# A gated cross-attention and mixture-of-experts layer: 512-byte table entries, written by token column, and a table cleared in five pieces from ScalarE's queue

## The chip, the cores and the metric

The kernel runs on one core of one Trainium2 chip. The metric is the device time of one execution in microseconds (us). The time before is the median of three runs. Beside them stands one profiled execution, from which all durations and waits are read.

## The reference, cut to what matters

There are 8 batches of 512 tokens with 256 features, so 4096 tokens. A layer norm and a masked cross-attention with 16 heads are added to `x` through a tanh gate. Then each token is normalised again, sent to its two best of eight experts, and their outputs, weighted by the router's probabilities, are added through a second gate.

```python
x = x + jnp.tanh(g_xattn[0]) * _L0_xattn_ref(_layernorm(x), ctx, ctx, mask, ...)
# the feed-forward part, on the result:
probs = jax.nn.softmax(x_flat @ router_w + router_b, axis=-1)
top_w, top_idx = jax.lax.top_k(probs, 2)
for e in range(8):
    h = jax.nn.gelu(x_flat @ expert_up[e].T, approximate=False)
    output = output + comb[:, e:e+1] * (h @ expert_down[e].T)
x = x + jnp.tanh(g_ffn[0]) * output
```

## The kernel before

The kernel computes only the chosen experts. It keeps a table in DRAM that lists, expert by expert, which tokens an expert has to process. `LINES` is 300 lines of 128 entries, 38,400 entries in all. An entry holds three numbers that matter (`FIELDS = 3`: the token to write to, the token to read from, its weight) and is padded to `ENTRY` 32-bit words, 16 before, so 64 bytes.

**Clearing.** `clear_table` (L158) fills a tile in SBUF with empty entries (three memsets on GpSimd, L161 to L163) and writes it over the whole table with one DMA from SyncE's queue (L165): 1536 pieces of 1600 bytes, 2400 KB. In the path that this input takes (`attend_near`) it is called at step `b == -1` (L1214) with a tile of tag "raw".

**The steps of the attention part.** `attend_near` goes through `b` from -1 to 7. In step `b` it computes the attention of batch `b` (`weights_T`, `weigh`: matmul, exponential on ScalarE, matmul), finds the score maxima of batch `b + 1` (`find_tops`), projects and normalises what comes next (`project`: `n_xnT`, `k`, `q` on ScalarE), and finishes batch `b - 1`. Each step has four groups `g` with three positions `n`; the dictionary `plan` says which piece of work goes where.

**Entering.** For every batch, `place` (L366) works out on GpSimd where in the table each token of the batch goes. It also fills `entries[:, b % 2]` for all four token columns and both choices at once: one copy (L391) and one multiplication (L394). Then `enter(t)` (L399) issues two indirect DMAs (L401), one for each choice of token column `t`; that is 8 per batch and 64 in all. There are two such buffers, so the entries of a batch may be overwritten once the DMAs of the batch two before have landed.

**The experts.** A job takes up to 256 rows of one expert. `list_rows` (L807) reads two table lines from DRAM, `fetch` (L843) gathers the token rows with indirect DMAs on GpSimd (`xg`), `turn` transposes them, `go_up` and `go_down` do the matmuls, `fetch_y` gathers the rows of the output that exist already (`y`), and L903 scatters the sum back to `out`. The first four jobs run inside steps 5 to 7; the others follow the attention part, and the last two batches' entries are made among them.

**What sets the order.** Each engine works through its own queue in order, but the order of a queue is not the order of the code. The program is built by a scheduler that follows the dependencies and lets an instruction whose inputs are ready go ahead of earlier written ones that still wait. `tc.keep_in_program_order(ins)` pins one instruction behind whatever was written last for its engine. Most vector and many ScalarE instructions carry such a pin; the instructions of `clear_table` and of `enter` do not. Every DMA issued from SyncE or ScalarE takes one of eight completion semaphores in turn and waits, on the engine that issues it, for the semaphore's last user.

The places that the change and the prediction name: `entries` L154, `clear_table` L158, `place` L366, `enter` L399, `plan_pairs` L672 with its line L686, `load_x` L89, `load_window` L510, the step loop L1209, and `attend_anywhere` (the path not taken here).

Of the kernel before, what the change touches and what calls it, by code (L numbers as in the profile page):

```python
# [11 lines left out]
F32 = mybir.dt.float32  # L12
# [8 lines left out]
P = 128  # L21
# [30 lines left out]

LINES = E * SHARE + 2 * SIZES[3]

ENTRY = 16
FIELDS = 3
JOBS = [(k, n) for k in range(2) for n in range(SIZES[k])]
for _n in range(OFTEN):
# [10 lines left out]
def flamingo_layer(ctx: ExitStack, tc: tile.TileContext, a: dict, out: bass.AP):  # L69
# [6 lines left out]
    def fixed(shape, name, dtype=F32):  # L76
        return const.tile(shape, dtype, tag=name, name=name)
# [73 lines left out]
    tokens_i = fixed([P, B * QT], "tokens_i", I32)  # L151
    nc.gpsimd.iota(tokens_i, pattern=[[P, B * QT]], base=0, channel_multiplier=1)

    entries = fixed([P, 2, QT, 2, ENTRY], "entries", I32)  # L154
    nc.gpsimd.memset(entries, 0)
    place_i = fixed([P, B * QT, 2], "place_i", I32)

    def clear_table(t):  # L158

        many = t.rearrange("p (n c) -> p n c", c=ENTRY)[:, : LINES // 12]  # L160
        nc.gpsimd.memset(many, 0)  # L161
        nc.gpsimd.memset(many[:, :, 0], TOKENS)
        nc.gpsimd.memset(many[:, :, 1], TOKENS - 1)  # L163
        n = many.shape[1]
        nc.sync.dma_start(  # L165
            out=table.rearrange("(p r n) c -> p r (n c)", p=P, n=n),
            in_=t[:, : n * ENTRY].unsqueeze(1).to_broadcast([P, LINES // n, n * ENTRY]),
        )


    lower = fixed([P, E + 1, E], "lower")
# [88 lines left out]
    def shared(p2, small, bank):  # L260
# [40 lines left out]
        def finish(b):  # L301

            x2T = p2.tile([P, DC, S], F32, tag="xnT", name=f"x2T{b}", bufs=1)
            said = {}

            def t3(name, dtype=F32):
                return small.tile([P, QT, E], dtype, tag=name, name=f"{name}{b}", bufs=2)

            def t2(name):
                return small.tile([P, QT], F32, tag=name, name=f"{name}{b}", bufs=2)  # L310

            def keep_rows(xn):
                nc.sync.dma_start(out=token_rows(rows, b), in_=xn)

            def keep_x():
                nc.sync.dma_start(out=token_rows(out, b), in_=xs[b])

            def logits():

                ps = bank(f"route_ps{b}")[:, :P]  # L320
                for dc in range(DC):
                    for t in range(QT):
                        nc.tensor.matmul(
                            ps[32 * t : 32 * t + 32, :], lhsT=rw[:, dc, :], rhs=x2T[:, dc, t * P : (t + 1) * P],
                            start=(dc == 0), stop=(dc == DC - 1),
                        )
                said["lgT"] = small.tile([P, P], F32, tag="lgT", name=f"lgT{b}", bufs=1)
                nc.scalar.copy(said["lgT"], ps)

            def route():  # L330
                ps = bank(f"lg_ps{b}")[:, :P]
                nc.tensor.transpose(ps, said["lgT"], ident)
                said["lg"] = t3("lg")
                nc.vector.tensor_tensor(
                    said["lg"], ps.rearrange("p (t e) -> p t e", t=QT)[:, :, :E], over_t(rb), ALU.add
                )

            def choose():
# [24 lines left out]
                nc.vector.tensor_tensor(both, picks[:, :, 0, :], picks[:, :, 1, :], ALU.add)  # L363
                said["top"], said["picks"], said["both"] = top, picks, both

            def place():  # L366

                both = said["both"].rearrange("p t e -> p (t e)")
                ps = bank(f"place_ps{b}")
                n = QT * E  # L370
                nc.tensor.matmul(ps[:, :n], lhsT=before, rhs=both, start=True, stop=True)
                nc.tensor.matmul(ps[:, n : 2 * n], lhsT=ones, rhs=both, start=True, stop=True)
                counts = small.tile([P, 2, QT, E], F32, tag="counts", name=f"counts{b}", bufs=2)
                nc.scalar.copy(counts.rearrange("p i t e -> p (i t e)"), ps[:, : 2 * n])
                place = t3("place")
                for t in range(QT):
                    nc.gpsimd.tensor_tensor(place[:, t, :], counts[:, 0, t, :], filled, ALU.add)
                    nc.gpsimd.tensor_tensor(filled, counts[:, 1, t, :], filled, ALU.add)
                mine = slice(b * QT, (b + 1) * QT)
                at = small.tile([P, QT, 2], F32, tag="at", name=f"at{b}", bufs=2)  # L380
                picked = said["picks"]
                nc.gpsimd.tensor_tensor(
                    picked, picked, place.unsqueeze(2).to_broadcast([P, QT, 2, E]), ALU.mult
                )
                for k in (4, 2, 1):
                    nc.gpsimd.tensor_tensor(
                        at.unsqueeze(3) if k == 1 else picked[..., :k], picked[..., :k], picked[..., k : 2 * k],
                        ALU.add,
                    )
                entry = entries[:, b % 2]  # L390
                nc.gpsimd.tensor_copy(  # L391
                    entry[:, :, :, :2], tokens_i[:, mine].unsqueeze(2).unsqueeze(3).to_broadcast([P, QT, 2, 2])
                )
                nc.gpsimd.tensor_scalar(  # L394
                    entry.bitcast(F32)[:, :, :, 2], said["top"][:, :, :2], tg[:, 1:2], None, ALU.mult
                )
                nc.gpsimd.tensor_copy(place_i[:, mine, :], at)

            def enter(t):  # L399
                for i in range(2):  # L400
                    nc.gpsimd.indirect_dma_start(  # L401
                        out=table_parts[2 * t + i][:, :],
                        out_offset=bass.IndirectOffsetOnAxis(ap=place_i[:, t, i : i + 1], axis=0),
                        in_=entries[:, b % 2, t % QT, i, :], in_offset=None,
                    )

            places = [place] + [lambda t=t: enter(t) for t in range(b * QT, (b + 1) * QT)]
            return x2T, keep_x, keep_rows, logits, route, choose, places

# [224 lines left out]
    def experts(pool, seen, half_bank, bank, row_bank):  # L634
# [8 lines left out]

        def open_wide():
            wide.append(pool("wide", 1))

        def halves(s):
            return 3 if JOBS[s][0] == 2 else 2
# [318 lines left out]
                    some(middle, len(JOBS))  # L967

        plan_steps = [plan_full(0), plan_full(1), plan_rest]
        return plan_steps, open_wide, list_rows, fetch, load, turn, ups, fetch_y, downs, compute, compute_extra  # L970


    def attend_near(att):
# [6 lines left out]
        def bank(name):  # L980
            return ps_g.tile([P, 512], F32, tag="g", name=name)

        plans, open_wide, list_rows, fetch, load, turn_rows, ups, fetch_y, downs, compute, compute_extra = experts(
            pool, [b * S for b in (*PARTS, B)], lambda name: ps_s.tile([P, 512], F32, tag="s", name=name), bank,
            lambda name: ps_o.tile([P, 512], F32, tag="av", name=name),
        )
# [222 lines left out]
        for b in range(-1, B):  # L1209
# [1 line left out]
                load_x(b + 3, p2)  # L1211
                load_win(b + 3)
            if b == -1:
                clear_table(p2.tile([P, S], I32, tag="raw", name="none", bufs=1))  # L1214
            behind_route = list(later)
            later.clear()
            if b == 0:
# [13 lines left out]
                        plan[where].append(step)  # L1231
            for g in range(4):
                c, i = g // 2, g % 2
                if b >= 0:
                    pT = weights_T(b, c, i)
                work = deque(amid.get((b, g), []))
# [39 lines left out]
    def attend_anywhere(att):  # L1276
# [70 lines left out]
        for t in vals:  # L1347
            nc.gpsimd.memset(t[:, :, :, DH:], 1.0)
        load_ctx(0)
        clear_table(p2.tile([P, S], I32, tag="raw", name="none"))  # L1350

# [184 lines left out]
    with which.Else():  # L1536
        with ExitStack() as att:
            attend_anywhere(att)
        with ExitStack() as exp:
            pool = lambda name, bufs, **kw: exp.enter_context(tc.tile_pool(name=name, bufs=bufs, **kw))  # L1540
            ps_h, ps_g = pool("ps_h", 4, space=PSUM), pool("ps_e", 4, space=PSUM)
            plans, open_wide, list_rows, fetch, load, turn_rows, _, _, _, compute, compute_extra = experts(
                pool, [TOKENS] * (len(PARTS) + 1),
                lambda name: ps_h.tile([P, 512], F32, tag="h", name=name),
                *[lambda name: ps_g.tile([P, 512], F32, tag="e", name=name)] * 2,
# [57 lines left out]
```

## Time and profile before

| | |
|---|---|
| median of 3 runs | 787.48 us (787.28 to 788.8) |
| profiled execution | 819.79 us, its span 818.0 us |
| PE / DVE / ACT / POOL busy in the span | 755.2 / 409.0 / 261.7 / 312.3 us |
| DMA packets, bytes | 82728, 113.32 MB |
| table<-none (the clear), SyncE's queue | 1 issue, 2400 KB |
| table<-entries (the entering) | 64 indirect DMAs, 62.8 us of GpSimd |

Times are from the span's start. PE is the matrix engine, DVE the vector engine, ACT ScalarE, POOL GpSimd and SP SyncE; SPq and ACTq mark what the queue of SP or ACT itself executes, such as issuing a DMA. A number in brackets with an arrow is the idle time of the engine before an instruction and what ended it. The profiled execution is 32 us longer than the median of the timed runs (819.79 against 787.48).

### The profile page before, as it was taken

To read this page: it belongs to the slowest core of one execution; us is meant where nothing else is said; L and a number is where in the kernel's file an instruction comes from. 1 tells how busy PE (TensorE), PEld (TensorE's weight loads), DVE (VectorE), ACT (ScalarE), POOL (GpSimd) and SP (SyncE) were. 2 spreads that over 40 slices of the span, in tenths; PEclk is the share of its full clock that TensorE was granted. 3 is DMA by queue.
4 is the path that set the end of the run, shared out by engine and by line. 5 is a ranking of instruction groups with operands and counts; after the bars stand their busy time and mean duration, and the time that the engine had idled before them with its cause. 6 is when DMAs were issued, how large, how long until landed. Compare 5 with 4: busy or idle time off the path is not lost. (4 is left out here: it accounts for less than half of the span.)

```text
span 818.0 us, 11151 instructions
## 1 busy us (share of the span) xinstructions
PE 755.2 (92%) x3898; PEld 544.3 (67%) x3898; DVE 409.0 (50%) x1315; ACT 261.7 (32%) x491; POOL 312.3 (38%) x420
## 2 busy tenths in 40 slices
PE   8999988888898989998799999999999999999992
PEld 3544534334465646677488888888788788878872
DVE  8898894958573575532053453524343423523300
ACT  4665654544553535422211112121211221121110
POOL 2020133333536151636563444344443444344331
PEclk9999997987998999999899999999999999999997
DMA  5700110100572230157436557575754654655310
GB/s 165 264 2 33 58 53 30 53 4 28 197 282 93 78 120 14 54 158 246 157 113 208 210 192 243 171 249 179 246 174 151 212 199 152 194 205 179 99 52 25
DMA packets 82728, 113.32 MB, mean 139 GB/s; under 512 B 16605, under 2 KB 67552, under 8 KB 82656
## 3 DMA queue, kind: packets, MB, share of 16 engines
q1 hardware_dynamic: 70000, 85.16, 31.4%
q0 software_dynamic: 11840, 26.76, 9.9%
q8 instruction: 35, 0.57, 0.3%
q10 hardware_dynamic: 816, 0.53, 0.2%
q14 instruction: 37, 0.30, 0.1%
HBM read 92.66 MB, written 20.28 MB: 138 GB/s over the span
## 5 line engine op out<-in xcount | busy, mean ns | idle before, releaser
L879 PE MATMUL h_ps<-xT,up 128*128 128x256 f32 (+1 forms) x1024 | 248.0, 398 | 7.6 <-issue 3.8
L897 PE MATMUL o_ps<-down,hT 128*128 128x256 f32 x1088 | 242.4, 380 | 4.9 <-DVE y L900 4.9
L897 PEld LDWEIGHTS o_ps<-down,hT 128*128 128x128 f32 x1088 | 205.4, 190 | 40.2 <-DVE y L900 6.8
L879 PEld LDWEIGHTS h_ps<-xT,up 128*128 128x128 f32 x1024 | 195.3, 192 | 52.6 <-issue 9.3
L868 DVE STREAM_TRANSPOSE xT<-xg 32x128 f32<-32x128 f32 (+1 forms) x368 | 115.6, 314 | 179.3 <-DMA xg<-rows,listed 167.7
L883 ACT ACTIVATE hT<-h_ps 128x512 f32<-128x512 f32 (+1 forms) x144 | 82.0, 573 | 342.7 <-PE h_ps L879 321.3
L903 POOL DMA_INDIRECT out<-y,listed x68 | 68.5, 1007 | 157.9 <-DVE y L900 133.8
L831 POOL DMA_INDIRECT y<-out,listed x68 | 65.0, 956 | 80.9 <-DMA out<-y,listed 53.8
L1038 DVE TENSOR_REDUCE tops<-t_ps 128x4 f32<-128x512 f32 x128 | 79.4, 683 | 25.8 <-PE t_ps L1033 15.1
L831 POOL DMA_INDIRECT xg<-rows,listed x68 | 66.3, 975 | 40.7 <-issue 18.6
L1068 ACT ACTIVATE n_pT<-w_ps 128x512 f32<-128x512 f32 x128 | 67.4, 602 | 39.0 <-PE w_ps L1063 35.6
L401 POOL DMA_INDIRECT table<-entries,place_i x64 | 62.8, 982 | 20.7 <-issue 16.2
L900 DVE SCALAR_TENSOR_TENSOR y<-o_ps,listed,y 128x256 f32<-128x256 f32 x68 | 31.1, 481 | 75.5 <-PE o_ps L897 51.4
L1063 PE MATMUL w_ps<-ql,km 32*128 32x512 f32 x256 | 54.1, 686 | 0.0
L1015 POOL TENSOR_TENSOR x<-x,bo 128x1024 f32<-128x1024 f32 x8 | 18.8, 2348 | 67.5 <-DVE bo L1014 38.9
L1087 DVE STREAM_TRANSPOSE raw<-n_av 128x512 f32<-128x512 f32 x32 | 22.8, 711 | 42.3 <-PE n_av L1081 19.6
L1033 PE MATMUL t_ps<-k,q 32*128 32x256 f32 x512 | 40.6, 416 | 0.3 <-ACT k L560 0.3
L1081 PE MATMUL n_av<-n_pT,nv 128*32 128x512 f32 x256 | 37.4, 659 | 2.7 <-DVE xT L856 2.7
L1033 PEld LDWEIGHTS t_ps<-k,q 32*128 32x128 f32 x512 | 25.5, 190 | 17.2 <-issue 11.8
L573 PE MATMUL q_ps<-n_xnT,wqT 128*128 128x512 f32 x64 | 32.4, 632 | 0.9 <-ACT n_xnT L286 0.6
L1102 PE MATMUL proj_ps<-woT,oT 128*128 128x256 f32 x128 | 31.4, 387 | 0.0
L1102 PEld LDWEIGHTS proj_ps<-woT,oT 128*128 128x128 f32 x128 | 23.4, 190 | 8.6 <-DVE st_f_a L225 3.4
(220 smaller groups left out, 538.6 us busy)
## 6 DMA issues: line engine op xcount, KB each, us to landing
up<-in_upT SPq DMA_DIRECT2D x32, 1024.0 KB
down<-in_downT SPq DMA_DIRECT2D x32, 1024.0 KB
out<-x SPq DMA_DIRECT2D x8, 512.0 KB
rows<-xn_f SPq DMA_DIRECT2D x8, 512.0 KB
x<-in_x SPq DMA_DIRECT2D x7, 512.0 KB
table<-none SPq DMA_DIRECT2D x1, 2400.0 KB
xg<-rows,listed POOLq DMA_INDIRECT x68
y<-out,listed POOLq DMA_INDIRECT x68
```

The source lines that it names most:

```text
L401: nc.gpsimd.indirect_dma_start(out=table_parts[2 * t + i][:, :], out_offset=bass.IndirectOffsetOnAxis(ap=place_i[:, t, i : i + 1], axis=0) ...
L831: ins = nc.gpsimd.indirect_dma_start(out=dst, out_offset=None, in_=src[: seen[JOBS[s][0]], :], in_offset=bass.IndirectOffsetOnAxis(ap=list ...
L868: nc.vector.transpose(dst[32 * g : 32 * g + 32, i], src[32 * i : 32 * i + 32, g])
L879: nc.tensor.matmul(ps[:, i, :], lhsT=up[:, dc, (f + i) * P : (f + i + 1) * P], rhs=xT[:, dc, :], start=(dc == 0), stop=(dc == DC - 1),)
L883: nc.scalar.activation(made[s][:, f : f + m, :], ps, AF.Gelu)
L897: nc.tensor.matmul(ps, lhsT=hT[:, f, h * P : (h + 1) * P], rhs=down[:, f, :], start=(f == 0), stop=(f == FC - 1))
L903: ins = nc.gpsimd.indirect_dma_start(out=out_parts[h][:, :], out_offset=bass.IndirectOffsetOnAxis(ap=listed[:, n, h, 0:1], axis=0), in_=y[ ...
L1033: ins = nc.tensor.matmul(ps[j][:, u], lhsT=q[rows_j, c, t * P : (t + 1) * P], rhs=k[rows_j, c], start=True, stop=True)
L1038: nc.vector.tensor_reduce(top[:, 2 * tp : 2 * tp + 2, :].rearrange("p t (i x) -> p t i x", i=2)[:, :, :, 32 * j], ps[j], AX.X, ALU.max,)
L1063: ins = nc.tensor.matmul(ps[j], lhsT=km[rows_j, c, i, :], rhs=lowered[b, c][rows_j, i, :], start=True, stop=True)
L1068: nc.scalar.activation(pT[:, j, :], ps[j], AF.Exp)
L1102: nc.tensor.matmul(ps[:, t - ts[0], :], lhsT=outs[b, c][:, t * P : (t + 1) * P], rhs=w["woT"][:, c, :], start=(c == 0), stop=(c == DC - 1),)
```

## The change

The entries become 128 words (512 bytes), so the table grows from 2.46 to 19.66 MB. `entries` has one buffer for each of the two choices instead of two for whole batches, and the copy and the multiplication are made in `enter`, for one token column and one choice at a time. `clear_table` now returns six steps: one that fills the tile (4 entries to a partition, 2 KB) and five that each issue a DMA of 3.93 MB, 1920 pieces of 2 KB. In `attend_near` they go to ScalarE's queue: the fill and the first piece are written at step -1, and one further piece at the beginning of each of the four groups of step 0, ahead of `weights_T`. None of them is pinned. The tile has the tag "xT" of the experts' pool instead of "raw".

```diff
-ENTRY = 16
+ENTRY = P
...
-    entries = fixed([P, 2, QT, 2, ENTRY], "entries", I32)
+    entries = fixed([P, 2, ENTRY], "entries", I32)
...
-    def clear_table(t):
-
-        many = t.rearrange("p (n c) -> p n c", c=ENTRY)[:, : LINES // 12]
-        nc.gpsimd.memset(many, 0)
-        nc.gpsimd.memset(many[:, :, 0], TOKENS)
-        nc.gpsimd.memset(many[:, :, 1], TOKENS - 1)
-        n = many.shape[1]
-        nc.sync.dma_start(
-            out=table.rearrange("(p r n) c -> p r (n c)", p=P, n=n),
-            in_=t[:, : n * ENTRY].unsqueeze(1).to_broadcast([P, LINES // n, n * ENTRY]),
-        )
+    def clear_table(t, queue):
+
+        many = t.rearrange("p (n c) -> p n c", c=ENTRY)
+        n, steps = many.shape[1], 5
+        runs = LINES // n // steps
+        parts = table.rearrange("(p k r n) c -> p k r (n c)", p=P, k=steps, n=n)
+
+        def fill():
+            nc.gpsimd.memset(t, 0)
+            nc.gpsimd.memset(many[:, :, 0], TOKENS)
+            nc.gpsimd.memset(many[:, :, 1], TOKENS - 1)
+
+        def put(k):
+            queue.dma_start(out=parts[:, k], in_=t.unsqueeze(1).to_broadcast([P, runs, n * ENTRY]))
+
+        return [fill, *(lambda k=k: put(k) for k in range(steps))]
...
-                entry = entries[:, b % 2]
-                nc.gpsimd.tensor_copy(
-                    entry[:, :, :, :2], tokens_i[:, mine].unsqueeze(2).unsqueeze(3).to_broadcast([P, QT, 2, 2])
-                )
-                nc.gpsimd.tensor_scalar(
-                    entry.bitcast(F32)[:, :, :, 2], said["top"][:, :, :2], tg[:, 1:2], None, ALU.mult
-                )
                 nc.gpsimd.tensor_copy(place_i[:, mine, :], at)
 
             def enter(t):
                 for i in range(2):
+                    nc.gpsimd.tensor_copy(entries[:, i, :2], tokens_i[:, t : t + 1].to_broadcast([P, 2]))
+                    nc.gpsimd.tensor_scalar(
+                        entries.bitcast(F32)[:, i, 2:3], said["top"][:, t % QT, i : i + 1], tg[:, 1:2], None, ALU.mult
+                    )
                     nc.gpsimd.indirect_dma_start(
...
-                        in_=entries[:, b % 2, t % QT, i, :], in_offset=None,
+                        in_=entries[:, i, :], in_offset=None,
                     )
...
+        def no_token():
+            return gather.tile([P, S], F32, tag="xT", name="none", bufs=2).bitcast(I32)
...
             if b == -1:
-                clear_table(p2.tile([P, S], I32, tag="raw", name="none", bufs=1))
+                clear = deque(clear_table(no_token(), nc.scalar))
+                clear.popleft()()
+                clear.popleft()()
...
             for g in range(4):
                 c, i = g // 2, g % 2
+                if b >= 0 and clear:
+                    clear.popleft()()
                 if b >= 0:
                     pT = weights_T(b, c, i)
```

The remaining lines of the diff pass `no_token` out of `experts` and let the other path issue its six steps at once on SyncE's queue.

More of the change, by code (lines that the diff above doesn't have):

```diff
@@ L969, in experts @@
         plan_steps = [plan_full(0), plan_full(1), plan_rest]
-        return plan_steps, open_wide, list_rows, fetch, load, turn, ups, fetch_y, downs, compute, compute_extra
+        return plan_steps, no_token, open_wide, list_rows, fetch, load, turn, ups, fetch_y, downs, compute, compute_extra
     def attend_near(att):
@@ L981, in bank @@
             return ps_g.tile([P, 512], F32, tag="g", name=name)
-        plans, open_wide, list_rows, fetch, load, turn_rows, ups, fetch_y, downs, compute, compute_extra = experts(
+        plans, no_token, open_wide, list_rows, fetch, load, turn_rows, ups, fetch_y, downs, compute, compute_extra = experts(
             pool, [b * S for b in (*PARTS, B)], lambda name: ps_s.tile([P, 512], F32, tag="s", name=name), bank,
@@ L1349, in attend_anywhere @@
         load_ctx(0)
-        clear_table(p2.tile([P, S], I32, tag="raw", name="none"))
+        for step in clear_table(p2.tile([P, S], I32, tag="raw", name="none"), nc.sync):
+            step()
         mask_i = load_mask(p2)
@@ L1541, in flamingo_layer @@
             ps_h, ps_g = pool("ps_h", 4, space=PSUM), pool("ps_e", 4, space=PSUM)
-            plans, open_wide, list_rows, fetch, load, turn_rows, _, _, _, compute, compute_extra = experts(
+            plans, _, open_wide, list_rows, fetch, load, turn_rows, _, _, _, compute, compute_extra = experts(
                 pool, [TOKENS] * (len(PARTS) + 1),
```

## The prediction, made before the changed kernel was seen

> **What bounds the kernel now.** I read the page first (engines, slices, the chain that ended last), then, since the change acts early and on queues, the timelines of ACT and SP from 18 to 62 us, busy time by stretch, and POOL's timeline at each batch of table entries.
>
> ```profile
> PE 755.2 (92%) x3898; PEld 544.3 (67%) x3898; DVE 409.0 (50%) x1315; ACT 261.7 (32%) x491; POOL 312.3 (38%) x420
> PE  8999988888898989998799999999999999999992
> ```
>
> PE is busy nearly everywhere. What stops PE for some us is not made up later: no later slice has idle time to give back. In the chain that ended last PE holds 11%; the rest is out and y DMAs and POOL of the last jobs, far from this change. What matters is whether the edit stops something that feeds PE.
>
> ```profile
> 22.46 2.07 ACT L275 ACTIVATE xn_a<-x,shift_a,rstd_end_a 128x256 f32<-128x256 f32 x4
> 24.70 0.37 ACT L546 COPY kn<-kv_ps 128x256 f32<-128x256 f32 x1 [0.16 <-PE kv_ps L542]
> 24.96 0.48 ACT L547 ACTIVATE nv<-kv_ps,kept 128x256 f32<-128x256 f32 x1
> 26.50 1.07 ACT L286 COPY n_xnT<-xnT_ps_a 128x512 f32<-128x512 f32 x2 [1.05 <-PE xnT_ps_a L285]
> 29.50 1.50 ACT L560 ACTIVATE k<-k_ps,bks,half 128x128 f32<-128x128 f32 x4 [1.93 <-PE k_ps L554]
> 33.49 0.69 ACT L577 ACTIVATE q<-q_ps,bqs 128x512 f32<-128x512 f32 x1 [2.48 <-PE q_ps L573]
> 37.63 2.04 ACT L1068 ACTIVATE n_pT<-w_ps 128x512 f32<-128x512 f32 x4
> ```
>
> This is ACT in step -1. It waits for PE by 1 to 2.5 us at a time, and PE waits for what ACT delivers (n_xnT, k, q): a chain in lockstep. The short holes are where an early-ready ACT instruction can slip in.
>
> ```profile
> 19.40 0.66 SPq L165 DMA_DIRECT2D table<-none  x1
> 20.16 3.64 SPq L92 DMA_DIRECT2D x<-in_x  x1
> 24.07 1.84 SPq L512 DMA_DIRECT2D win<-in_ctxT  x1
> 26.02 1.67 SPq L92 DMA_DIRECT2D x<-in_x  x1
> 24.00:29.00 5.00, 5.00 (x44) 3.24 (x43) 4.31 (x8) 2.36 (x6) 0.00 (x0) 1.00 1.06 383
> 29.00:34.00 5.00, 4.89 (x32) 2.82 (x31) 5.00 (x10) 2.02 (x5) 0.00 (x0) 1.00 1.09 374
> 37.00:60.00 23.00, 22.76 (x156) 11.18 (x152) 19.49 (x57) 16.22 (x34) 4.69 (x2) 1.00 0.02 7
> ```
>
> The first four lines are SP's queue, the last three the stretches (columns: PE, PEld, DVE, ACT, POOL, clock, DMA share, GB/s). The clear moves at some 375 GB/s with all DMA engines full; from 37 to 60 us they are nearly idle. The issue of the clear itself took 0.66 us, but the issue of the x load behind it took 3.64 instead of the 0.38 that the same load takes with an empty queue (18.25). By the packet records, that issue ended when some 103 earlier pieces per DMA engine were outstanding, the four after it at 79 to 97. So an issue returns once about 100 pieces per engine or fewer lie ahead, and until then its engine stands still. For SP that costs nothing.
>
> ```profile
> L686 DVE TENSOR_SCALAR line<-iota_e x3: 163/165/174, 21.9 to 419.8; 128x9 f32<-128x9 f32 x3
> ```
>
> This unpinned line belongs to a plan whose next operations (L669, L709) run at 197 us. Its first execution is at 21.9: the build puts unpinned instructions whose inputs are ready into the first hole, 175 us ahead of their place in the code.
>
> **The change part by part.**
>
> *The clear on ACT.* A piece has 1920 parts of 2 KB, 120 per DMA engine; at 375 GB/s its 3.93 MB take 10.5 us, and all five 52. The pieces need only the fill on POOL (17.2 us before), so by the L686 row I expect pieces 1 to 4 not in the four groups of step 0 but in ACT's first holes of step -1, behind nv or n_xnT. Piece 0 is written before the pinned xn_a, so it stays ahead of it: at 22.5, 0.66 us. Its data start about 25[...] and share the engines with 2.5 MB of x and window loads, which begin at about 20.3 and no longer queue behind the clear. Piece 1, issued at about 26, returns once 20 parts per engine of piece 0 are through. Each further one returns a piece later: piece 4 when 480 - 100 = 380 parts per engine are done, 12.45 MB; with the loads 14.95 MB, or 39.9 us at 375 GB/s. That is 60 us. ACT makes n_xnT then instead of at 26.5: 34 us lost. Queued behind it are n_xnT, k, q and the exponentials of batch 0; PE stops at k_ps (28.75), as both banks that it could use hold n_xnT's inputs, and DVE stops after the tops it has been given. About 1 us comes back, since DVE's backlog is cleared: +33.
>
> Here a rule speaks to it. The Trainium skill, "DMA: Bandwidth & Descriptors", section "Issuing engines are not separate DMA queues", says that issuing from several engines adds no bandwidth and saves only issue time, which it calls usually small relative to the DMA. By the rule the five issues cost ACT 5 x 0.66 = 3.3 us and the sum would be some 6; by the row of 3.64 us it is 33. I take the row: the pieces are larger than what fits.
>
> *SP without the clear.* The x load at 20.16 goes out 0.7 us earlier and its data up to 7 us earlier. No early PE wait is on x, so 0. The "raw" tile is first needed at 44.5, long after the old clear: 0. Later loads share engines with the clear until about 80 us; of SP's there are one window at 39 and at 68 and the out store at 76.9, none near its deadline: 0, up to +1. ACT's own semaphore waits are for loads that are done by 28.
>
> *Entering.*
>
> ```profile
> 127.29 0.95 POOL L401 DMA_INDIRECT table<-entries,place_i  x1 [0.30 <-DMA table<-entries,place_i]
> 129.72 0.20 POOL L391 COPY entries<-tokens_i 128x16 int32<-128x16 int32 x1 [1.47 <-DMA table<-entries,place_i]
> 428.15 0.99 POOL L903 DMA_INDIRECT out<-y,listed  x1 [0.30 <-issue]
> 438.89 0.48 DVE L900 SCALAR_TENSOR_TENSOR y<-o_ps,listed,y 128x256 f32<-128x256 f32 x1 [1.03 <-DMA y<-out,listed]
> ```
>
> An indirect DMA takes 1.26 us of POOL with the gap, eight a batch 10.1. Now each has a copy (nearest row 0.20) and a multiplication (nearest 0.32 for 8 elements, I take 0.30) ahead, with 0.08 between: 0.66 more, 5.3 per batch, less the 0.5 removed: +4.8, in all 38 us of POOL's 818. The new wait: a copy may overwrite `entries[:, i]` only when the DMA of the column before has landed. The second line shows landing within 1.47 us of the last issue; the other choice's turn in between takes 1.9, so the wait is 0 with quiet DMA, and 1 to 3 us per column when weights stream (the y gathers in the chain land in 2.7 to 3.4). For batches 0 to 3 POOL has idle stretches of 5 us or more behind the entries. For batches 6 and 7 the out and xg DMAs stand behind them: the out at 428.15 went out when POOL got to it, and the y gather behind it arrived 1 us late for DVE (last line). Jobs alternate, so most of a 5 us delay is absorbed: between 0 and +10, I take +2.
>
> *512-byte entries.* The gain of wider writes can only be POOL's waits for landed entries, 6.5 us in five places, none of which PE waits for; `listed` reads the same 12-byte pieces, and POOL waits for them 10.6 us in two places. Bound -3 to +1, taken as 0.
>
> Sum: 33 + 2 = +35, on a profiled execution of 819.8. The stall is set by DMA bytes, not by the matrix clock, so it carries over whole to the median: 787.5 + 35 = 822.
>
> **The rivals.**
>
> *The pieces stay in their places* (one per group of step 0, near 37.5, 43, 50 and 57 us). Then piece 2 finds about 78 parts ahead and returns at once, piece 3 finds 116 and waits 1 us, piece 4 133 and waits 2.5. With 5 x 0.6 us of issue that is 6.5, of which ACT's holes there hide 1 to 2: +5, with entering +7: 794.5. For it: the code says so. Against: the L686 row.
>
> *An issue on ACT does not stop ACT*, or its queue holds more than SP's. Then 3 us of issue, mostly in holes, and the entering: +2, 789.5. Against: the first ACT activity comes right behind its three issues at the start.
>
> *Faster.* Nothing blocks, and the wider entries are listed sooner: the 2.4 and 8.2 us that POOL waits for `listed` shrink, and the 2.53 us that PE waits for xT at 371 goes. At most -3: 784.5. It decides only if ACT is stopped for under 1 us and POOL's extra 4.8 per batch are covered.
>
> *Not what it says:* if the build took the five pieces to overlap in the table, each would wait for the one before to land. The two weight loads into interleaved halves of `wkv` went out 0.4 us apart without such a wait, so I give it little; it would look like the first rival with waits of up to 12 us where ACT is early: +5 to +15.
>
> **How the numbers follow.** ACT blocked in step -1: 0.60, at 822, own range 812 to 831 (a piece or two in later holes saves up to 10, entering costs up to 8 more). Pieces in place or chained: 0.24, 790 to 803. No block: 0.11, 787 to 791. Faster: 0.05. The range 789 to 831 leaves out the faster case, half of "no block" and the tail of the first. 0.2% (1.6 us) is about what a measurement of this kernel can tell from no change; faster by more than that 0.05, within it 0.05, slower 0.90.
>
> **What would show it.** On ACT's queue five issues of table<-none between 22 and 60 us, three of some 10 us each; n_xnT of step -1 at about 60; PE and DVE empty in slices 2 and 3; DMA full until about 80. Entering: L401 at a pitch near 1.9 us. It is wrong if the issues are short, if they stand among the exponentials of step 0, or if PE's idle time has moved behind 350 us, where only entering could cause it.

## The result and the profile after

The changed kernel took 821.32 us (817.21 to 823.11) where the kernel before took 787.79 (787.28 to 788.8): a ratio of 1.0417, 95% interval 1.0373 to 1.0461. That is 33.5 us slower; the forecast was 822. The total came out, but the experiments split it differently from the forecast: roughly half is the clear (13 to 16 us) and half the entering (16 to 19), which was to cost 2 us. The record does not say on which chip these runs were made, which matters further down.

From the page of the changed kernel (the same lines of the kernel before stand in the prediction):

```profile
span 820.9 us, 11245 instructions
PE 751.1 (91%) x3898; PEld 544.4 (66%) x3898; DVE 411.7 (50%) x1315; ACT 259.7 (32%) x491; POOL 342.1 (42%) x532
PE   8789989898799899999758999999999999999992
```

Slices 2 and 3 are not empty, as they were to be; they lose a tenth or two. The one hole worth the name is the 7 and the 5 in slices 20 and 21, around 407 us, where the forecast had almost nothing.

Next the timeline of ACT from 22 us on, with the lines left out that bear on nothing here:

```profile
22.30 0.41 ACTq L171 DMA_DIRECT2D table<-none  x1
22.84 2.07 ACT L280 ACTIVATE xn_a<-x,shift_a,rstd_end_a 128x256 f32<-128x256 f32 x4 [0.48 <-issue]
26.47 0.59 ACT L291 COPY n_xnT<-xnT_ps_a 128x512 f32<-128x512 f32 x1 [0.93 <-PE xnT_ps_a L290]
26.48 3.94 ACTq L171 DMA_DIRECT2D table<-none  x1
30.46 0.59 ACT L291 COPY n_xnT<-xnT_ps_a 128x512 f32<-128x512 f32 x1 [3.41 <-issue]
40.14 1.00 ACTq L171 DMA_DIRECT2D table<-none  x1
41.19 1.27 ACT L579 ACTIVATE q<-q_ps,bqs 128x512 f32<-128x512 f32 x2 [8.73 <-issue]
44.56 6.49 ACTq L171 DMA_DIRECT2D table<-none  x1
51.41 1.08 ACT L1073 ACTIVATE n_pT<-w_ps 128x512 f32<-128x512 f32 x2 [3.63 <-PE t_ps L1038]
52.29 8.29 ACTq L171 DMA_DIRECT2D table<-none  x1
60.63 1.51 ACT L562 ACTIVATE k<-k_ps,bks,half 128x128 f32<-128x128 f32 x4 [6.19 <-PE t_ps L1038]
```

An issue does hold ACT: four of its instructions stand for 3.41, 8.73, 3.63 and 6.19 us, 22 in all, and the last issue returns at 60.58, as was worked out. (The brackets of the last two name PE, but each starts within 0.4 us of an issue's return: 44.56 + 6.49 = 51.05 and 52.29 + 8.29 = 60.58.) But ACT did its work between the issues. Piece 1 stands between the two copies of n_xnT, piece 2 in front of q, pieces 3 and 4 among the exponentials of step 0. The stretches of the forecast, read again (same columns):

```profile
24.00:29.00 5.00, 5.00 (x44) 3.26 (x43) 4.30 (x8) 2.12 (x5) 0.00 (x0) 1.00 1.08 385
29.00:34.00 5.00, 3.33 (x27) 2.07 (x27) 3.82 (x7) 2.00 (x5) 0.00 (x0) 1.00 1.06 401
37.00:60.00 23.00, 20.17 (x108) 9.75 (x107) 14.14 (x49) 9.63 (x20) 2.36 (x1) 0.93 1.05 407
```

The DMA engines are full to the end of the third line, yet PE is busy for 20.17 of its 23 us.

Now the entering of batch 6 on POOL, with what follows it:

```profile
388.43 0.18 POOL L399 COPY entries<-tokens_i 128x2 int32<-128x2 int32 x1 [3.30 <-DMA table<-entries,place_i]
388.60 0.30 POOL L400 TENSOR_SCALAR entries<-top,tg 128x1 f32<-128x1 f32 x1
389.18 1.08 POOL L403 DMA_INDIRECT table<-entries,place_i  x1 [0.28 <-POOL entries L400]
390.28 0.19 POOL L399 COPY entries<-tokens_i 128x2 int32<-128x2 int32 x1
...
402.36 1.03 POOL L908 DMA_INDIRECT out<-y,listed  x1 [0.16 <-issue]
403.69 1.00 POOL L908 DMA_INDIRECT out<-y,listed  x1 [0.30 <-issue]
411.55 0.98 POOL L836 DMA_INDIRECT y<-out,listed  x1 [6.85 <-DMA out<-y,listed]
```

The pitch of L403 is 1.8 to 1.9 us, as forecast, and the copies waited for landings in places (3.30 here). Behind the columns come the write of out and the gather of y that needs it. PE pays, in the waits of PE and DVE from 365 to 430 us:

```profile
PE o_ps L902 <- DVE y L905: 13.5, 1, 13.5
DVE count L674 <- POOL filled L383: 22.0, 1, 22.0
```

`count` is the first instruction of the plan for the last batches. It reads `filled`, which the last placing on POOL writes, and that placing stands behind the gather of y. The addition of y, for which PE waits, stands behind `count` in DVE's queue.

**The profile of before is not the one to compare with.** Its execution was 32 us over its median. Set beside it, the changed kernel is 2.9 us longer (820.9 against 818.0), and its cost cannot be seen. The first experiment gave a profile of the same kernel at its usual time (span 786.4). The rows of the granted clock of the two executions of the kernel before, the one on record first, and then of the changed kernel:

```profile
PEclk9999997987998999999899999999999999999997
```

```profile
PEclk9999999997999999999989999999999999999996
```

```profile
PEclk9998998798989999999969999999999999999996
```

By the clock records behind these rows PE had half its clock for 51, 24 and 58 us before the tail. Against the second one the changed kernel's 34.5 us of span split into 13.3 more busy time of PE (751.1 against 737.8 for the same 3898 matmuls, with 34 us more at half clock) and 21.2 more idle time (69.8 against 48.6).

### The profile page after: what moved, and what is told of

The parts are those of the page before. It is cut to its first block, busy times and chain, and to the rows that moved or that the text cites. A ratio compares the mean times of both kernels' runs of the same rounds, so it can differ in the third digit from the quotient of the medians.

```text
span 820.9 us, 11245 instructions
## 1 busy us (share of the span) xinstructions
PE 751.1 (91%) x3898; PEld 544.4 (66%) x3898; DVE 411.7 (50%) x1315; ACT 259.7 (32%) x491; POOL 342.1 (42%) x532
## 5 line engine op out<-in xcount | busy, mean ns | idle before, releaser
L902 PE MATMUL o_ps<-down,hT 128*128 128x256 f32 x1088 | 246.6, 385 | 20.4 <-DVE y L905 20.4
L902 PEld LDWEIGHTS o_ps<-down,hT 128*128 128x128 f32 x1088 | 208.3, 193 | 57.0 <-DVE y L905 22.2
L884 PE MATMUL h_ps<-xT,up 128*128 128x256 f32 (+1 forms) x1024 | 242.8, 393 | 3.1 <-DVE tops L1043 2.2
L884 PEld LDWEIGHTS h_ps<-xT,up 128*128 128x128 f32 x1024 | 193.3, 190 | 44.8 <-DVE tops L1043 2.6
L403 POOL DMA_INDIRECT table<-entries,place_i x64 | 66.5, 1039 | 19.4 <-POOL entries L400 13.3
L1068 PE MATMUL w_ps<-ql,km 32*128 32x512 f32 x256 | 52.2, 717 | 0.0
L1038 PE MATMUL t_ps<-k,q 32*128 32x256 f32 x512 | 43.2, 416 | 0.3 <-ACT k L562 0.3
L1038 PEld LDWEIGHTS t_ps<-k,q 32*128 32x128 f32 x512 | 27.3, 190 | 18.2 <-issue 12.8
L575 PE MATMUL q_ps<-n_xnT,wqT 128*128 128x512 f32 x64 | 33.5, 647 | 3.2 <-ACT k L562 1.8
L400 POOL TENSOR_SCALAR entries<-top,tg 128x1 f32<-128x1 f32 x64 | 19.5, 307 | 28.1 <-DVE top L358 28.0
```

The lines of the kernel that those rows point to most:

```text
L403: nc.gpsimd.indirect_dma_start(out=table_parts[2 * t + i][:, :], out_offset=bass.IndirectOffsetOnAxis(ap=place_i[:, t, i : i + 1], axis=0) ...
L884: nc.tensor.matmul(ps[:, i, :], lhsT=up[:, dc, (f + i) * P : (f + i + 1) * P], rhs=xT[:, dc, :], start=(dc == 0), stop=(dc == DC - 1),)
L902: nc.tensor.matmul(ps, lhsT=hT[:, f, h * P : (h + 1) * P], rhs=down[:, f, :], start=(f == 0), stop=(f == FC - 1))
L1038: ins = nc.tensor.matmul(ps[j][:, u], lhsT=q[rows_j, c, t * P : (t + 1) * P], rhs=k[rows_j, c], start=True, stop=True)
L1068: ins = nc.tensor.matmul(ps[j], lhsT=km[rows_j, c, i, :], rhs=lowered[b, c][rows_j, i, :], start=True, stop=True)
```

## The experiments

Four groups were run, each on another chip, and each is compared with the kernel before on its own chip. The chips are of two kinds. The kernel before took 788.7 in the first group and 788.1 in the fourth, but 820.9 in the second and 820.4 in the third.

### First group (before: 788.7): which half costs what

*The kernel before once more*, for a profile at its usual time.

> The kernel before, unchanged, to get a second profile and the granted clock of its timed runs. In the first profile (819.8 us against 787.5 for the timed runs) the matrix clock was at half speed for some 51 us before the last tail, in eight stretches. If half-clock stretches are what separates the two, the timed runs have a mean clock near 0.99 and a profile near 787 us has fewer than 15 us of them; then the changed kernel's 821 us may be, in part, half-clock time that the change brings on. If the timed runs have a clock of 0.96 as well, the clock explains nothing and the 32 us lie elsewhere.

788.44, ratio 1.0001 (0.9978 to 1.0023). The mean clock of its runs was 0.97 to 0.98 and its trace has 24 us at half clock, between the two cases expected. Its trace is the measure below.

*The clear alone.* The kernel before, with its own clear and entries, and beside them the five large pieces on ACT's queue, written to a table that nobody reads (so 2.4 MB more to write than in the changed kernel):

```diff
+    spare = tc.dram_tile([LINES * P, P], I32, name="spare")
...
             if b == -1:
+                clear = deque(clear_spare(no_token(), nc.scalar))
+                clear.popleft()()
+                clear.popleft()()
...
+                if b >= 0 and clear:
+                    clear.popleft()()
```

> The kernel before with its old clear, its 64-byte entries and its old entering, and besides them the five pieces of the changed kernel (same size, same places in the code, ScalarE's queue), written to a spare table that nobody reads. Theory ACT (the issues stop ScalarE and that is the whole loss): about 820 us. Theory TWO (the stopped issues cost what the two profiles show by step 1, 10.7 us, and the entering the rest): 797 to 800 us. If issues on ScalarE cost nothing: 788.

804.94, ratio 1.0186 (1.0134 to 1.0238): +16.2, between the two expectations and nearer to TWO. Piece 1 stands where it stood in the changed kernel, between the two copies of `n_xnT`, but what holds it is another thing:

```profile
26.46 0.58 ACT L302 COPY n_xnT<-xnT_ps_a 128x512 f32<-128x512 f32 x1 [0.88 <-PE xnT_ps_a L301]
43.87 0.38 ACTq L183 DMA_DIRECT2D spare<-none  x1
44.30 0.58 ACT L302 COPY n_xnT<-xnT_ps_a 128x512 f32<-128x512 f32 x1 [17.25 <-DMA spare<-none]
```

This standstill is not the one of the forecast. Piece 1's issue itself takes 0.38 us. It was held back until piece 0 had landed, 21.5 us after its issue at 22.37, because the semaphore that it waits for is the one that piece 0's landing raises: in this trace pieces 0 and 1 have the same one of the eight, in the changed kernel's pieces 0 and 2. The second half of n_xnT stands behind it in ACT's queue, and PE stops for 15.51 us (29.43 to 44.94). The 8.73 us in front of q in the changed kernel is the same thing: piece 2 goes out at 40.14, when piece 0, issued at 22.30, had landed (17.8 us). Piece 1 was then still under way (issued at 26.48, landed 23.6 us later), so the pieces are not chained each to the one before.

*The entering alone.* Entries of 64 bytes, the old clear, the new `enter`:

```diff
-    entries = fixed([P, 2, QT, 2, ENTRY], "entries", I32)
+    entries = fixed([P, 2, ENTRY], "entries", I32)
...
                 for i in range(2):
+                    nc.gpsimd.tensor_copy(entries[:, i, :2], tokens_i[:, t : t + 1].to_broadcast([P, 2]))
+                    nc.gpsimd.tensor_scalar(
+                        entries.bitcast(F32)[:, i, 2:3], said["top"][:, t % QT, i : i + 1], tg[:, 1:2], None, ALU.mult
+                    )
```

> The kernel before with its 64-byte entries and its one clear from SyncE, but with the entering of the changed kernel: a copy and a multiplication per column and choice, two one-entry buffers. Theory ACT: 788 to 790 us. Theory TWO (GpSimd gets so late at batches 6 and 7 that the vector engine waits for `filled` and the matrix engine for a bank): 800 to 812 us, with one matrix-engine gap of over 10 us between 380 and 430 us.

808.06, ratio 1.0226 (1.0144 to 1.0309): +19.4, as TWO had it. Theory ACT falls here. With +16.2 for the clear the parts make 35.6, where 33.5 was measured, so they nearly add. As the clear alone stood ACT still in another way than in the changed kernel, its 16.2 is not quite the clear's share there; taking the entering alone from the whole leaves 13.3 (821.32 less 808.06). The gap was where TWO put it, and as long as in the changed kernel:

```profile
PE o_ps L894 <- DVE y L897: 16.3, 2, 13.7
DVE count L666 <- POOL filled L378: 22.2, 1, 22.2
```

*The pieces on SP.* The changed kernel with its pieces on the queue that had them before:

```diff
-                clear = deque(clear_table(no_token(), nc.scalar))
+                clear = deque(clear_table(no_token(), nc.sync))
```

> The changed kernel with the five pieces on SyncE's queue; GpSimd's order is the same. Theory ACT: 788 to 792 us, unless the x loads queued behind the pieces come late. Theory TWO: the 10.7 us of the early steps go and the rest stays, 808 to 812 us.

814.86, ratio 1.0314 (1.0263 to 1.0364): 3 us above TWO's range and far from ACT's 788 to 792. The start is clean (the first proj matmul of batch 0 at 67.72, in the kernel before 69.16), but two pieces now stand ahead of a load of x:

```profile
37.06 20.69 SPq L171 DMA_DIRECT2D table<-none  x2
57.80 9.48 SPq L92 DMA_DIRECT2D x<-in_x  x1
67.47 2.38 SPq L514 DMA_DIRECT2D win<-in_ctxT  x1
```

SP stood 20.69 and 9.48 us, and DVE waited 5.6 us for that x. The 19.7 MB hold up something in either queue.

Where the time goes, by the start of a few landmarks on PE (us; "before" is the trace of the first experiment):

| start of | before | changed | clear alone | entering alone | pieces on SP |
|---|---|---|---|---|---|
| first proj of batch 0 | 69.16 | 80.08 | 86.68 | 67.63 | 67.72 |
| first h of job 0 | 214.10 | 234.20 | 234.27 | 219.46 | 227.37 |
| first h of job 7 | 369.18 | 391.33 | 389.22 | 375.90 | 383.41 |
| first o of job 6 | 385.02 | 420.10 | 405.21 | 404.94 | 412.33 |
| first o of the last main job | 764.34 | 798.09 | 783.73 | 783.54 | 792.02 |

The clear costs the changed kernel 10.9 by batch 0. From 24 us to that landmark PE does the same matmuls in both; it is idle for 7.2 us of the stretch instead of 0.6 and busy for 48.9 instead of 44.6, at a mean granted clock of 0.91 instead of 0.96. So 6.6 of the 10.9 are waits and 4.3 are slower matmuls. The entering alone costs 5.4 by job 0 (PE waits 5.9 us for that job's gathered rows, `xg`, in the kernel before 1.9), 6.7 by job 7, and 13 more up to the next landmark, at the gap. After 440 us little changes.

### Second group (before: 820.9): which mechanism

*Small pieces.* The kernel before with its 64-byte table cleared in five pieces on ACT, at the places of the changed kernel:

```diff
-        n, steps = many.shape[1], 5
+        n, steps = 30, 5
+        t = t[:, : n * ENTRY]
```

> The kernel before with its entries of 64 bytes and its entering by batch, but the table cleared in five pieces on ScalarE's queue, at the places of the changed kernel, each piece an eighth of the bytes (256 rows of 1,920 bytes in place of 1,920 rows of 2,048). Theory VOLUME (ScalarE stands because 19.7 MB has to drain before the next issue is taken): every issue is under 1.5 us, ScalarE's copies stand under 2 us, and the time is 787 to 792. Theory PLACE (it is enough that the issues stand in ScalarE's queue, where a piece waits for the completion of an earlier one): 798 to 806, with standstills of several us at piece 1 or 2 as with the large pieces.

827.9 against 820.91, ratio 1.0102 (1.0037 to 1.0167). Both theories are half right:

```profile
22.35 0.41 ACTq L172 DMA_DIRECT2D table<-none  x1
23.07 0.40 ACTq L172 DMA_DIRECT2D table<-none  x1
29.60 0.38 ACTq L172 DMA_DIRECT2D table<-none  x1
30.02 0.37 ACT L552 COPY kn<-kv_ps 128x256 f32<-128x256 f32 x1 [5.06 <-DMA table<-none]
30.07 0.42 ACTq L172 DMA_DIRECT2D table<-none  x1
30.54 1.07 ACTq L172 DMA_DIRECT2D table<-none  x1
```

With an eighth of the bytes the issues take 0.4 to 1.1 us, so the long ones (3.9 to 8.3) came from volume. (Bytes and number of parts fell together; which of the two counts is not told apart.) What is left is the wait of the third piece for an earlier piece's landing: 5.06 us in front of kn, and PE stops for 4.34 there.

*An entry for every column.*

```diff
+                    entry = entries[:, b % 2, t % QT, i]
-                    nc.gpsimd.tensor_copy(entries[:, i, :2], ...)
+                    nc.gpsimd.tensor_copy(entry[:, :2], ...)
```

> Entering by token column as in the changed kernel, entries of 64 bytes, the clear as before, but every column of the two batches in flight has an entry of its own, as in the kernel before, in place of one that all columns share. The same number of small GpSimd instructions; only the wait for the scatter that last read the entry is gone. Theory WAIT (the column waits for its predecessor's landing): a batch is entered in about 10 us again and the time is 787 to 793. Theory COUNT (96 more small instructions on GpSimd are the price): 800 to 808, as with the shared entry.

821.44, ratio 1.0013 (0.9994 to 1.0031). The absolute figures expected were for the other kind of chip. The trace answers part of it. The waits of POOL's copies for landings, in the changed kernel from 100 to 425 us and here from 100 to 420:

```profile
POOL entries L399 <- DMA table<-entries,place_i: 16.9, 13, 3.5
POOL entries L395 <- DMA table<-entries,place_i: 0.6, 2, 0.3
```

The waits are all but gone, the small instructions are drawn ahead, and batch 6's eight DMAs start from 382.81 to 391.77 us, one every 1.28, as in the kernel before. So the wait and the order it enforces stretch a batch, not the number of instructions. What that is worth in time was not settled here, since on this kind of chip a kernel that does wait is no slower either, as the next run shows.

*`count` kept in its order.* In the entering alone DVE stood at `count` for 22.2 us with the additions of y behind it. Here this one instruction stays behind them:

```diff
-            nc.vector.scalar_tensor_tensor(count, iota, -float(SHARE * P), filled, ALU.mult, ALU.add)
+            (tc.keep_in_program_order if k == 2 else id)(nc.vector.scalar_tensor_tensor(count, ...))
```

> Entering by token column with the shared entry, entries of 64 bytes, the clear as before (808.06 when it was run), and one instruction of VectorE kept in its program order: the first of the plan for the last batches, `count`, which reads GpSimd's `filled`. It then stands behind the additions of the outputs (y) instead of ahead of them. Theory COUNT-WAIT (VectorE stands at `count` for 22 us while the accumulators wait behind it, and this is the last 12 us of the loss): TensorE's gap of 13.7 us at o_ps is gone, 794 to 799. Rival LATE-GATHER (the late gather of y would stop VectorE anyway): the gap stays at y itself, 804 to 809.

806.84, where before took 820.91 on this chip: 0.9878 (0.9812 to 0.9944). The ratio says nothing of `count` alone, as the entering alone was not run on this chip. The waits do:

```profile
PE o_ps L894 <- DVE y L897: 15.3, 2, 7.8
DVE y L897 <- DMA y<-out,listed: 20.6, 3, 19.3
```

PE still stops for 15.3 us, now in two pieces. COUNT-WAIT falls: the row named `count`, but without it DVE waits at the next thing that POOL is late with, the gather of y.

*The same in the kernel before.*

> The kernel before with the same one instruction (`count`) kept in its program order. In the undisturbed profile of the kernel before VectorE waits 9.0 us at it and TensorE has a gap of 5.85 us at 399. COUNT-WAIT: that gap goes, 781 to 785. LATE-GATHER: no change, 786 to 790.

817.26, ratio 0.9956 (0.9929 to 0.9983): 3.7 us faster, but the 5.85 us gap that it aimed at does not occur in this kernel on this kind of chip, so it decides nothing on COUNT-WAIT.

### Third group (before: 820.4): the change on the other kind of chip, and POOL's order

> The changed kernel as it is, once more. The kernel before took 788.7 in the first group of experiments and 820.9 in the second, which ran on another chip, with 24 and (in the profile on record) 51 us at half clock. Theory ADD (the change's own delays come on top, whatever the chip): 1.04 times the kernel before of this group, 819 to 824 where that is at 788, 850 to 857 where it is at 820. Theory SHARED (the stretches at half clock that the one chip adds and the ones that the change brings are the same holes, filled once): where the kernel before is at 820 the changed one is within 1% of it, 818 to 829.

The changed kernel took 814.65, ratio 0.9954 (0.9923 to 0.9984). ADD falls; the size fits SHARED (0.5% faster where within 1% was expected), whose mechanism was not tested. The verdict "4% slower" belongs to the chips on which the kernel before takes 788: beside the result itself, whose chip is not on record, the first group shows it, where the clear alone, the entering alone and the changed kernel with its pieces on SP were all slower. The change's own marks are all there in this trace: standstills of ACT of 3.87, 8.94, 3.64 and 6.18 us and a gap of 12.58 us at o_ps, 401.60 to 414.18. What is missing is what the kernel before loses there and the changed one does not. In the profile on record the kernel before started job 7's first matmul at 407.73, on the fast kind of chip at 369.18; the changed kernel starts it at 386.32 here and had it at 391.33.

*Batch 6 entered behind the last placing.* The changed kernel with

```diff
-        first = [lambda: choice(route, choose), place, *enter]
+        first = [lambda: choice(route, choose), place]
...
-        spread = [step for one in enter_last for step in (one, wait, wait)]
+        spread = [step for one in enter for step in (one, wait)] + enter_last
```

and the instructions of batch 6's `enter` kept in their order.

> The changed kernel with the entering of the last batch but one (batch 6) put behind the placing of the last one and kept there, so that on GpSimd the write of out, the gather of y and the last placing no longer stand behind its eight columns of 2 us. Keeping `count` in its order did not take TensorE's gap away: it moved to y's gather itself (19.3 us). Theory LATE-GATHER: the gap of 13.5 us at o_ps near 407 goes, or shrinks to under 5; 9 to 14 us less than the changed kernel of this group. Rival ELSEWHERE (the later columns hold up the next gathers just the same): the gap comes back within 40 us, and the time is within 4 us of the changed kernel.

819.5, against 814.65 of the changed kernel on the same chip: 4.9 us slower. LATE-GATHER was right about the gap it named, which is gone, and wrong about the time; ELSEWHERE, which allowed 4 us either way, was nearly right about it. At the first o of job 7 this kernel is 18 us ahead of the changed one (415.78 against 434.09), and at the next job's first o the lead is down to 1.5:

```profile
PE o_ps L903 <- DVE y L906: 18.3, 1, 18.3
DVE xT L874 <- DMA xg<-rows,listed: 28.7, 1, 28.7
```

Now the gather of xg is late, as it stands behind the moved columns. POOL's queue is full here; putting another DMA first only picks the victim.

*The same step in the kernel before.*

> The kernel before with the same step: the entering of batch 6 behind the placing of the last batch. Its profile has a gap of 5.85 us at o_ps where the batch stands ahead of the gather of y. Theory LATE-GATHER: 3 to 6 us under the kernel before, where that is at 788; ELSEWHERE: within 2 us of it, or slower.

822.49, ratio 1.0051 (1.0019 to 1.0082), so no gain either.

### Fourth group (before: 788.1): the queue, tested by an undoing in part

The first six batches by column with one shared entry, the last two by batch:

```diff
+                if b >= B - 2:
                     entry = entries[:, b % 2]
...
+                    entry = entries[:, b % 2, t % QT, i] if b >= B - 2 else entries[:, 1, QT - 1, i]
+                    if b < B - 2:
+                        nc.gpsimd.tensor_copy(entry[:, :2], tokens_i[:, t : t + 1].to_broadcast([P, 2]))
```

> Entries of 64 bytes and the clear as before; the first six batches are entered by token column with one shared entry, as in the changed kernel, the last two by batch, as in the kernel before. Moving batch 6 behind the placing (the run before) only moved TensorE's stop from the gather of y to the gather of xg, 18.3 us at 430, so it is GpSimd's queue there that is full. Theory QUEUE (the price of entering by column is what the last two batches' columns of 2 us push back on GpSimd's queue): the gap of 13.7 us near 391 shrinks to the 6 of the kernel before, and only the 5 to 7 us of steps 2 and 4 are left: 792 to 798, on either kind of chip, so slower than the kernel before by 1% where that takes 788 and faster by 3% where it takes 820. Rival SPREAD (the columns of the earlier batches have used the lead up already): the gap stays, 804 to 809.

795.88, ratio 1.0098 (1.0066 to 1.013): QUEUE, in the middle of its 792 to 798. The waits of PE and DVE from 370 to 430 us, and below them those of the kernel before (first experiment, 365 to 430):

```profile
PE o_ps L904 <- DVE y L907: 6.7, 2, 5.7
DVE count L676 <- POOL filled L378: 9.4, 1, 9.4
PE o_ps L897 <- DVE y L900: 6.4, 2, 5.9
DVE count L669 <- POOL filled L378: 9.0, 1, 9.0
```

The long gap is back to the size that it has in the kernel before. So 12.2 of the entering's 19.4 us (808.06 less 795.88, two chips of the same kind) belong to the columns of the last two batches, and 7.8 (795.88 less 788.07) to the six before them. At the first o of job 6 the mixed kernel is 9.4 us behind the kernel before, the entering alone 19.9.

No kernel beat both on the fast kind of chip. On the other kind the entering by column with `count` in its order did (806.84; its ratio of 0.9878 lies under the changed kernel's 0.9954, the two on different chips). The mixed kernel was not run there.

## Why the prediction was right in its total and wrong in its split

**An issue stops ACT, and the last one returns at 60 us: right.** It returned at 60.58. Forecast and trace also agree that the DMA engines stay full to nearly 80 us (the last data of the clear were written at 78.6). The measure of "about 100 pieces per engine" held too: by the packet records the issues of pieces 1 to 4 returned with 86 to 89 parts of earlier pieces outstanding per engine. The row of 3.64 us told the truth against the rule of the Trainium skill ("DMA: Bandwidth & Descriptors", section "Issuing engines are not separate DMA queues") that issue time is usually small beside the DMA: the five issues of the changed kernel take 20.1 us (0.41, 3.94, 1.00, 6.49, 8.29), not 3.3. Small pieces brought them back to 0.4 to 1.1.

**Pieces 1 to 4 go into ACT's first holes of step -1: the step that failed, for half of them.** The L686 row showed that an instruction can float 175 us ahead; it does not say that every one floats. Pieces 3 and 4 stood among the exponentials of step 0, which the forecast had named as a sign that it is wrong. n_xnT was copied at 26.47 and 30.46, not at 60.

**+33 for the clear: mis-sized.** The clear alone measured +16.2, and in the changed kernel 13.3 are left for it. There PE is 10.9 us late by batch 0, only 6.6 of it waits, out of 22 us of standstills of ACT: with the pieces spread, ACT delivers between two of them, and PE is busy for 20.17 of the 23 us from 37 to 60. The forecast took the whole drain as one block with ACT silent.

**"ACT's own semaphore waits are for loads that are done by 28", put at nothing: wrong.** Piece 2 waited for the semaphore of piece 0, which landed at 40.1. That, and not a full queue, was ACT's longest standstill, 8.73 us in the changed kernel and 17.25 with the clear alone. That an issue waits for its semaphore's last user was known before the forecast, but the pieces were not counted among the users; a chain was thought of only for the case that the pieces were taken to overlap in the table.

**SP without the clear, 0: not contradicted.** SP's early issues, 0.38 to 0.69 us, are short; its first load behind the old clear had taken 3.64.

**Entering, +2 of a range of 0 to 10: the other step that failed.** The measure is +19.4, outside its own bounds. The prices of a column were right (0.18 and 0.30 us, a pitch of 1.8 to 1.9, waits up to 3.5). What failed is the sentence "most of a 5 us delay is absorbed". The forecast spoke of 5 us behind batch 6. The DMAs of batch 6 start over 18.1 us (380.21 to 398.29, with two gathers of xg in between), in the kernel before over 9.0 (356.72 to 365.69), and the chain behind them has no slack: out, its landing, y, the last placing. It had stopped PE for 5.9 us already; the forecast could not see that, since the execution it was read from does not have this gap.

**512-byte entries, 0: not contradicted.** No run changed the size of the entries alone. The entries' DMAs land in a median 2.4 us and the lists in 5.0; with entries of 64 bytes and the same entering, 2.2 and 4.8.

**"Set by DMA bytes, not by the matrix clock, so it carries over whole to the median": right by luck.** The base was an execution 32 us over its median, and two errors of opposite sign, +17 at the clear and -17 at the entering, made up the rest. Nor is the stall free of the matrix clock: 4.3 of the 10.9 us by batch 0 are matmuls that ran slower, and over the whole span PE is busy 13.3 us longer. On the third group's chip the same sum would have been 40 us off. Of the rivals, the pieces in place (+5 for the clear) had the places of pieces 3 and 4 right and the size wrong.

**Still open:** why the kernel before loses 32 us on two of the four chips. Its profile on record (819.79 us, of a chip that is not named) and that of the first experiment agree to 0.25 us up to 122 us. Then, in the one on record, DVE is held by PE, in the waits of DVE from 119 to 132 us:

```profile
DVE tops L1038 <- PE route_ps L323: 4.3, 1, 4.3
DVE raw L1087 <- PE xnT_ps_f L285: 2.2, 1, 2.2
```

In the other execution it waits 0.5 for tops there. The clock records have half clock from 128.8 to 139.1 us in the first, none until 176 in the second. So PE is the engine on which the two part, and the one on record has 27 us more at half clock (51 against 24). But half clock alone does not explain the 32 us: at half speed 27 us cost at most 14, PE is also idle 14 us longer (62.8 against 48.6), and by the second routing matmul, at 128.26, it is already over 2 us late, before that half clock is recorded. What comes first, and why the kernels that enter by column with a shared entry lose less there, stays open.

## What to carry to other kernels

A large DMA issued from a compute engine can cost that engine more than a short issue: here it stood for up to 8.3 us while the queue was too full to take the request, and for 8.7 to 17 us when a request had to wait for an earlier one's landing. Look in the engine's timeline at what stands right behind each issue, and count which earlier DMA has its semaphore. A buffer shared by consecutive indirect DMAs turns their landing time into a wait in the issuing queue (16.9 us here); in this kernel most of the entering's price (12.2 of 19.4 us) was paid where that queue is already full, by whoever stands behind. Before summing on a profile, compare its time with the median; if they differ by more than the effect, find a profile that doesn't.

## What the runs showed of the hardware that was not expected

- The same program (the kernel before) took 788 us on two chips and 820 on two others, with no execution between 793 and 813, and the sign of a change's effect went with it: 1.0417 on record, 0.9954 on one of the slow two.
- A DMA of 0.38 us of issue held ACT for 17.25 us, because it had to wait for an earlier one to land. With pieces of 490 KB in place of 3.9 MB it was still 5.06.
- Entries of 512 bytes in place of 64 landed no sooner (2.4 against 2.2 us).
